# A four-layer hybrid network on one core: the head of the Mamba layer is shortened, and layer 1's contexts and queries of the first batch are computed beside the Mamba layer's scans of the second

## The chip, the core and the metric

The kernel runs on one core of a Trainium2 chip, in fp32 but for a few index matrices. The metric is the device time of one execution in microseconds (us), as the median of several runs. A profile of one further execution says where that time goes: TensorE is PE (its weight loads PEld), VectorE is DVE, ScalarE is ACT, GpSimd is POOL, and SP is the queue that starts most of the DMAs.

## What is computed

The input is x with 2 batches of 256 channels and 48 by 48 pixels, so each batch is a sequence of 2304 tokens. Four layers follow one another. Only the first two bear on this change:

```
layer 0:  h = layernorm(x) + pos;  xi, z = split(h @ in_proj)          # 512 channels each
          for each direction (forward, backward over the tokens):
            xs = silu(conv4(xi));  dt, B, C = xs @ xproj;  dt = softplus(dt @ dtproj + b)
            h_t = exp(dt_t * A) * h_(t-1) + dt_t * xs_t * B_t          # 16 states a channel
            y_t = <h_t, C_t> + D * xs_t
          x = x + ((y_f + y_b) * silu(z)) @ out_proj
layer 1:  t = groupnorm(x)                                            # over a whole batch
          q, k, v = t @ Wqkv + bqkv;  q = relu(q) / sqrt(32);  k = relu(k)
          ctx = k^T v  per head of 32 channels, over all tokens of the batch
          img = q @ ctx;  t = bn(t + proj(depthwise_conv3x3(img)))
          x = x + bn(t + mlp(t))                                      # 256 -> 2048 -> 256
```

Layer 2 is an attention and a graph-gated mixture of experts, and layer 3 is an attention and a routed mixture of experts. Neither is touched.

## The kernel before, in words

Everything lies channels by tokens: 128 partitions, two or four blocks of channels, and tokens in chunks of W = 384, six chunks to a batch. The residual `xres` stays in SBUF for the whole kernel.

**Layer 0** (`layer0`, L165 to L520) is a list `order` of 24 steps: batch 0 forward chunks 0 to 5, batch 0 backward 5 to 0, then the same for batch 1. I call them scans 0 to 23 after the function `scan` (L409) that does one. A scan goes over 4 blocks of channels and 16 states, 64 pairs in all. For each pair ACT makes exp(dt * A) in PSUM (L454), DVE runs the recurrence (L460 forward, L463 backward), DVE or POOL multiplies by C (L468), and PE adds the product into `yp` by a matmul with the identity (L422). POOL makes dt * xs * B for four states at once (L437), from `bb` and `cc`, which are broadcast from DRAM (L432, L434). The last value of each recurrence is copied into `state` (L470).

Before a chunk can be scanned, two things must have been done:

- `project_in(b, c)` (L204): layernorm of the chunk, position added, eight output blocks projected. Four go to `xi_d` in DRAM (L245), four to `z_d` (L247). It is a generator with 12 yields.
- `prepare(b, s, c, got)` (L288): loads the chunk with its neighbours from `xi_d` (L293, tile `xw`), does the short convolution as 16 matmuls with diagonal taps (L302), silu (L312), the projection to dt, B and C (L318), softplus as Abs and Relu, Exp, Ln and three additions on DVE (L335 to L348), and dt * xs on POOL (L350). It has 15 yields and hands its tiles over in `got`.

After a backward chunk, `project_out` (L354) multiplies by `w_out` and adds to `xres`. All of this is given to `scan` as `beside`, a list of (generator, steps, end): after every second pair, which is a slot (32 slots a scan), the generator is advanced so that `steps` of its yields are done by slot `end`. What the program writes is not yet the order of the queues: the builder puts each engine's instructions in an order of its own before the run, by the place in the program as a priority, and lets later work go ahead where earlier work isn't ready by its reckoning. The trace shows it: the statistics of batch 1 (L137), which stand in the program behind layer 1's fourth chunk, ran at 2441.7 us, at layer 1's start.

Beside scan i run `prepare` for scan i+1 (15 steps by slot 25), and in scans 0 to 9 also `project_in` of the chunks (0,2) to (1,5). In scans 10 to 21 there are instead three steps each of `head_products` (L367), products of layer 2's weights that only need PE and a little DVE; its 36 steps load weights (L377), multiply (L383, L397) and evacuate (L388, L390, L403 to L406). In scan 13 `group_stats` (L128) computes batch 0's groupnorm statistics. While scans run, all these helpers take their PSUM from `hold` (L199), which is one single buffer, tag "mm".

Before the first scan there is a head: `project_in` of chunks (0,0) and (0,1) in full, then `prepare` of the first chunk in full (L494 to L499). All twelve chunks of x are loaded at the start.

**Layer 1** (`layer1`, L544) does batch 0 and then batch 1. For each batch: `group_norm` (L592), the contexts over 18 token blocks (L608 to L621: K and V by PE, bias by DVE, relu by ACT, product into `cx`), then `image(c)` (L627: queries, and queries times context into the padded image `img`), `conv` (L646, nine taps on DVE), `project` (L664) and `mlp` (L683) for each chunk. `image` runs three chunks ahead. DVE fills its idle time there with `sort_list` (L895), which sorts layer 2's edges and belongs to nothing in layer 1.

Of the kernel before, what the change touches and what calls it, by code (L numbers as in the profile page):

```python
# [27 lines left out]
P = 128  # L28
# [4 lines left out]
W = 384  # L33
# [19 lines left out]
class Env:  # L53


    def __init__(self, ctx, tc, p):
        nc = self.nc = tc.nc
        self.tc, self.p, self.n_pools = tc, p, 0
        const = ctx.enter_context(tc.tile_pool(name="const", bufs=1))
        self.const = const  # L60
        self.dram = ctx.enter_context(tc.tile_pool(name="dram", bufs=1, space=DRAM))
        self.vec = const.tile([P, _NV], F32, name="vec")
        nc.sync.dma_start(self.vec, p["vecs"])
        self.ident = const.tile([P, P], F32, name="ident")
        make_identity(nc, self.ident)
        self.mean_c = const.tile([P, P], F32, name="mean_c")
        nc.vector.memset(self.mean_c, 1.0 / C)
        self.eps = {}
        for e in (1e-5, 1e-6):
            t = const.tile([P, 1], F32, name=f"eps{len(self.eps)}")  # L70
            nc.vector.memset(t, e)
            self.eps[e] = t
        self.xres = const.tile([P, 2, T], F32, name="xres")

        self.gmat = const.tile([P, P], F32, name="gmat")
        with tc.tile_pool(name="envw", bufs=1) as wp:
            same_block(self, wp, self.gmat, 3, 1.0 / 8)
        self.gn = const.tile([P, NB, 2, 2], F32, name="gn")

        self.gm_d = self.dram.tile([3, 2, P, 2 * C], F32, name="gm_d")  # L80
        self.ub = const.tile([P, 3, 2, 2], F32, name="ub")
# [45 lines left out]

def group_stats(E, wp, bank, b):  # L128

    nc = E.nc  # L130
    xb = E.xres[:, :, b * L : (b + 1) * L]
    gm, gr = E.gn[:, b, 0], E.gn[:, b, 1]
    mv = wp.tile([P, 2, 2], F32, tag="mv", name="mv")
    for k in range(2):
        st = wp.tile([P, NCH, 6], F32, tag="st", name="st")
        for c in range(NCH):
            nc.vector.bn_stats(st[:, c, :], xb[:, k, c * W : (c + 1) * W])  # L137
            yield
        nc.vector.bn_aggr(mv[:, k, :], st)
# [16 lines left out]
def load_x(E, b, c):  # L156
    xin = E.p["x"].rearrange("b (k p) n -> p b k n", p=P)
    E.nc.sync.dma_start(
        E.xres[:, :, b * L + c * W : b * L + (c + 1) * W], xin[:, b, :, c * W : (c + 1) * W]
    )  # L160
# [4 lines left out]
def layer0(ctx, E):  # L165
# [24 lines left out]
    nc.sync.dma_start(w_in, p["in_proj_wT"].rearrange("(k p) m -> p k m", p=P))  # L190
# [62 lines left out]
    for b in range(NB):  # L253
        for c in range(NCH):
            if (b, c) != (0, 0):
                load_x(E, b, c)
# [31 lines left out]
    def prepare(b, s, c, got):  # L288
# [39 lines left out]
        dt = wp.tile([P, DB, W], F32, tag="dt", name="dt")  # L328
        ex = up.tile([P, DB, W], F32, tag="ex", name="ex")
        for d in range(DB):  # L330
            pd = hold()
            nc.tensor.matmul(
                pd, lhsT=w_dt[s][:, d * P : (d + 1) * P], rhs=pr[0:16, :], start=True, stop=True
            )
            nc.scalar.activation(ex[:, d, :], pd, AF.Abs, bias=E.v(f"dt_b_{s}", d, 1))  # L335
            nc.scalar.activation(dt[:, d, :], pd, AF.Relu, bias=E.v(f"dt_b_{s}", d, 1))
            yield
        nc.scalar.activation(ex, ex, AF.Exp, scale=-1.0)
        dtu = wp.tile([P, DB, W], F32, tag="dtu", name="dtu")
        ln = up.tile([P, DB, W], F32, tag="ln", name="ln")  # L340
        nc.scalar.activation(dtu, ex, AF.Identity, bias=one[:, 0:1])
        yield
        nc.scalar.activation(ln, dtu, AF.Ln)
        nc.scalar.activation(dtu, dtu, AF.Identity, bias=one[:, 1:2])
        yield
        nc.vector.tensor_tensor(ex, ex, dtu, ALU.subtract)
        nc.vector.tensor_tensor(dt, dt, ln, ALU.add)
        nc.vector.tensor_tensor(dt, dt, ex, ALU.add)  # L348
        yield
        nc.gpsimd.tensor_tensor(dtu, dt, xs, ALU.mult)  # L350
        got.extend((b, s, c, xs, y, dt, dtu, bcd))
        yield
# [14 lines left out]
    def head_products():  # L367
# [3 lines left out]
        for h, m, z in [(h, m, z) for h in range(3) for m in range(2) for z in range(2)]:  # L371
# [35 lines left out]
            yield  # L407

# [85 lines left out]
    for steps in (first, project_in(0, 1)):  # L494
        for _ in steps:
            pass
    ready = []
    for _ in prepare(0, "f", 0, ready):
        pass  # L499
    scanning = True  # L500
    pieces = [(0, c) for c in range(2, NCH)] + [(1, c) for c in range(NCH)]
    after = None
    heads = head_products()
    for i, (b, s, step, c) in enumerate(order):
        now, ready = ready, []
        beside = [(after, 2, 5)] if after else []
        if i + 1 < len(order):
            nb, s2, _, c2 = order[i + 1]
            beside.append((prepare(nb, s2, c2, ready), 15, 25))
        if i < len(pieces):  # L510
            beside.append((project_in(*pieces[i]), 12, 32))
        elif i < len(pieces) + 12:
            beside.append((islice(heads, 3), 3, 32))
        if (b, s, step) == (1, "f", 1):

            beside.append((group_stats(E, up, lambda: hold()[:, 0:2], 0), 15, 32))
        scan(step, beside, *now)
        after = project_out(b, c, now[4]) if s == "b" else None
# [25 lines left out]
def layer1(ctx, E, edges):  # L544
# [4 lines left out]
    HD, NTB = 32, L // P  # L549
# [11 lines left out]
    wfc1 = big.tile([P, 2, 2048], F32, name="wfc1")  # L561
    nc.sync.dma_start(wfc1, p["Wfc1"].rearrange("(k p) m -> p k m", p=P))
    wfc2 = big.tile([P, 16, C], F32, name="wfc2")
    nc.sync.dma_start(wfc2, p["Wfc2"].rearrange("(k p) m -> p k m", p=P))

    hmask = big.tile([P, P], F32, name="hmask")
    same_block(E, lw, hmask, 5, HD**-0.5)

# [23 lines left out]
    def group_norm(b):  # L592
        if b:
            run(group_stats(E, wp, lambda: ps.tile([P, 2], F32, tag="mm", name="pg"), b))
        xb = E.xres[:, :, b * L : (b + 1) * L]
        for k in range(2):
            nc.vector.tensor_scalar(
                E.xn[:, k, b * L : (b + 1) * L], xb[:, k, :], E.gn[:, b, 0, k : k + 1],
# [3 lines left out]
    group_norm(0)  # L602
    for b in range(NB):
# [3 lines left out]
        cx = [psc.tile([P, P], F32, tag=f"cx{m}", name=f"cx{m}") for m in range(2)]  # L607
        for t in range(NTB):  # L608
            pk = ps.tile([P, 512], F32, tag="mm", name="pk")
            for k in range(2):  # L610
                nc.tensor.matmul(
                    pk, lhsT=xn[:, k, t * P : (t + 1) * P], rhs=wqkv[:, k, C:],
                    start=k == 0, stop=k == 1,
                )
            kv = wp.tile([P, 512], F32, tag="kv", name="kv", bufs=3)
            nc.vector.tensor_tensor(kv, pk, bkv, ALU.add)
            nc.scalar.activation(kv[:, :C], kv[:, :C], AF.Relu)
            for m in range(2):
                nc.tensor.matmul(
                    cx[m], lhsT=kv[:, m * P : (m + 1) * P], rhs=kv[:, C + m * P : C + (m + 1) * P],  # L620
                    start=t == 0, stop=t == NTB - 1,  # L621
                )
        cxm = wp.tile([P, 2, P], F32, tag="cxm", name="cxm")
        for m in range(2):
            nc.vector.tensor_tensor(cxm[:, m, :], cx[m], hmask, ALU.mult)

        def image(c):  # L627
# [97 lines left out]
        for c in range(3):  # L725
            image(c)
        t1 = project(0, conv(0))
        for c in range(NCH):
# [15 lines left out]
            if b + 1 < NB and c == NCH - 3:  # L744
                group_norm(b + 1)
# [1262 lines left out]
```

## Time and profile before

| what | us |
|---|---|
| median of the 3 runs shown (5373.67 to 5379.39) | 5376.03 |
| the profiled execution's own time | 5420.46 |
| its span, first to last instruction | 5418.6 |
| head: start to the first recurrence (L460) | 103.9 |
| scans 0 to 23: first recurrence to the last `y` (L427 starts 2426.6) | 2323 |
| layer 1: first context matmul (L611) to the last L710 | 2438.4 to 3132.1 |
| of it contexts of batch 0 and of batch 1 (L611) | 2438.4 to 2481.2, 2789.9 to 2836.0 |

In the profile's page, PE is busy for 88% of the span, DVE 65%, POOL 44%, ACT 44%. Read as one number for the whole kernel that says little: by slices, DVE and POOL are at 8 and 9 tenths during the scans (slices 1 to 17), POOL is idle in layer 1, and PE is at 9 tenths and above from there on. A matmul's end in this profile is modelled, so a busy PE isn't a PE at its peak. Weight loads overlap the matmuls.

### The profile page before, as it was taken

The page shows a single profiled execution, that of the slowest core. Times are in us where ns is not written, and L with a number is a line of the kernel's source. Part 1 is how long each engine was busy: PE and PEld are TensorE (multiplying, and loading weights), DVE is VectorE, ACT ScalarE, POOL GpSimd, SP SyncE. Part 2 cuts the span into 40 slices and gives each one's busy share as a digit, 9 for nine tenths or more (in the row PEclk, how much of TensorE's full clock was granted, in tenths as well). Part 3 has the DMA queues.
Part 4 walks back from the last instruction along what each step waited for, and adds up shares of the span by engine and source line. Part 5 has one row for each costly group of instructions (what it writes and reads, how often), then busy time and mean ns, then how long its engine had stood idle before and what let it go on. Part 6 is the DMA issues. An engine that isn't in the chain of part 4 may idle for free. (4 is left out here: it accounts for less than half of the span.)

```text
span 5418.6 us, 47326 instructions
## 1 busy us (share of the span) xinstructions
PE 4773.2 (88%) x15246; PEld 2642.9 (49%) x15246; DVE 3503.3 (65%) x5372; ACT 2370.0 (44%) x4939; POOL 2403.7 (44%) x1308
## 2 busy tenths in 40 slices
PE   7888888888787778879999989999799999999897
PEld 3444444444343344435555555556455455555675
DVE  4999888898999888899996244546534401212343
ACT  5767767666677666642223223422122222222111
POOL 2888888788888888880000000038502100000331
PEclk8999999999899899989999999999898999999899
DMA  4454454444454444431110000111121200000422
GB/s 152 166 177 173 164 178 170 159 162 151 160 174 158 173 166 158 148 137 61 33 45 6 1 16 0 40 29 30 15 72 52 61 7 9 6 9 6 83 83 94
DMA packets 185425, 499.13 MB, mean 92 GB/s; under 512 B 33382, under 2 KB 106474, under 8 KB 184906
## 3 DMA queue, kind: packets, MB, share of 16 engines
q1 hardware_dynamic: 176458, 483.23, 26.1%
q0 software_dynamic: 8704, 12.73, 1.6%
q8 instruction: 124, 2.03, 0.2%
q14 instruction: 139, 1.14, 0.1%
HBM read 422.73 MB, written 73.15 MB: 92 GB/s over the span
## 5 line engine op out<-in xcount | busy, mean ns | idle before, releaser
L422 PE MATMUL yp<-hc,ident 128*128 128x384 f32 x3072 | 1201.7, 523 | 253.2 <-DVE hc L468 210.9
L437 POOL TENSOR_TENSOR db<-dtu,bb 128x1536 f32<-128x1536 f32 x384 | 1329.1, 3462 | 64.6 <-DVE hs L463 21.0
L422 PEld LDWEIGHTS yp<-hc,ident 128*128 128x128 f32 x3072 | 576.2, 199 | 830.2 <-DVE hc L468 408.5
L468 POOL TENSOR_TENSOR hc<-ho,cc 128x384 f32<-128x384 f32 x576 | 584.9, 1023 | 189.9 <-DVE ho L460 82.6
L468 DVE TENSOR_TENSOR hc<-hs,cc 128x384 f32<-128x384 f32 x960 | 496.7, 537 | 57.9 <-PE yp L422 56.6
L454 ACT ACTIVATE hs<-dt,negab 128x384 f32<-128x384 f32 x768 | 435.9, 581 | 93.9 <-DVE hc L468 43.1
L454 ACT ACTIVATE hs<-dt,negaf 128x384 f32<-128x384 f32 x768 | 433.7, 581 | 65.0 <-DVE ho L460 28.8
L463 DVE TENSOR_TENSOR_SCAN hs<-hs,state,db 128x384 f32<-128x384 f32 x400 | 393.8, 1006 | 50.2 <-POOL db L437 23.8
L460 DVE TENSOR_TENSOR_SCAN hs<-hs,state,db 128x384 f32<-128x384 f32 x400 | 395.3, 1007 | 27.4 <-POOL db L437 19.6
L1813 POOL DMA_INDIRECT xe<-xt_d,token x48 | 47.4, 988 | 754.4 <-issue 715.3
L302 PE MATMUL mm<-xw,w_cv 128*128 128x384 f32 x768 | 292.4, 520 | 60.2 <-DVE xres L364 22.0
L1748 PE MATMUL po<-at,xtok 128*128 128x384 f32 x864 | 329.7, 506 | 8.2 <-ACT at L1746 8.1
L953 POOL PARTITION_ALL_REDUCE most<-most x1 | 0.4, 381 | 721.4 <-DVE mx L811 721.4
L1739 PE MATMUL sp<-qT,xn 128*128 128x384 f32 x864 | 317.2, 486 | 0.0
L1746 ACT ACTIVATE at<-sp 128x384 f32<-128x384 f32 x216 | 104.8, 491 | 473.1 <-PE sp L1739 473.0
L1395 PE MATMUL ph<-xn,w 128*128 128x384 f32 x768 | 287.0, 515 | 16.8 <-DMA y_d<-y 5.9
L1399 ACT ACTIVATE hid<-ph,vec 128x384 f32<-128x384 f32 x192 | 110.6, 581 | 337.2 <-PE ph L1395 244.6
L691 PE MATMUL pf<-t,wfc 128*128 128x384 f32 x768 | 255.3, 488 | 0.0
L710 PE MATMUL po<-hid,wfc 128*128 128x384 f32 x768 | 253.6, 486 | 0.0
L470 ACT COPY state<-hs 128x1 f32<-128x1 f32 x800 | 117.7, 155 | 293.6 <-DVE hc L468 291.7
L463 DVE TENSOR_TENSOR_SCAN ho<-hs,state,db 128x384 f32<-128x384 f32 x240 | 238.9, 995 | 10.3 <-ACT hs L454 10.2
L460 DVE TENSOR_TENSOR_SCAN ho<-hs,state,db 128x384 f32<-128x384 f32 x240 | 238.6, 994 | 7.0 <-ACT hs L454 6.6
(442 smaller groups left out, 7970.5 us busy)
## 6 DMA issues: line engine op xcount, KB each, us to landing
bb<-bcd SPq DMA_DIRECT2D x192, 768.0 KB
cc<-bcd SPq DMA_DIRECT2D x192, 768.0 KB
xw<-xi_d SPq DMA_DIRECT2D x24, 774.0 KB
w<-in_m_w SPq DMA_DIRECT2D x16, 1024.0 KB
y_d<-y SPq DMA_DIRECT2D x32, 384.0 KB
ye<-y_d SPq DMA_DIRECT2D x32, 384.0 KB
xi_d<-xz SPq DMA_DIRECT2D x48, 192.0 KB
z_d<-xz SPq DMA_DIRECT2D x48, 192.0 KB
```

The costliest lines, as they stand in the source:

```text
L302: nc.tensor.matmul(px, lhsT=w_cv[b, s][:, d * 4 + k, :], rhs=xw[:, d, o : o + W], start=k == 0, stop=k == 3,)
L422: nc.tensor.matmul(yp[d], lhsT=E.ident, rhs=hc, start=False, stop=summed[d] == NS)
L437: nc.gpsimd.tensor_tensor(db, bc(dtu[:, d, :], [P, GN, W], 1), bb, ALU.mult)
L454: nc.scalar.activation(hs, dt[:, d, :], AF.Exp, scale=nega[s][:, d * NS + n : d * NS + n + 1])
L460: nc.vector.tensor_tensor_scan(to, hs, db[:, j], init, ALU.mult, ALU.add)
L463: nc.vector.tensor_tensor_scan(to[:, ::-1], hs[:, ::-1], db[:, j, ::-1], init, ALU.mult, ALU.add)
L468: (nc.gpsimd if on_pool else nc.vector).tensor_tensor(hc, to, cc[:, j, :], ALU.mult)
L691: nc.tensor.matmul(pf, lhsT=wfc1[:, k, f * P : (f + 1) * P], rhs=t1[:, k, :], start=k == 0, stop=k == 1,)
L710: nc.tensor.matmul(po[m], lhsT=wfc2[:, f, m * P : (m + 1) * P], rhs=hid[:, i, :], start=f == 0, stop=f == 15,)
L1395: nc.tensor.matmul(ph, lhsT=w1[:, e, k, f * P : (f + 1) * P], rhs=xn[:, k, c * W : (c + 1) * W], start=k == 0, stop=k == 1,)
L1739: nc.tensor.matmul(sp, lhsT=xn[:, k, t0 + i * P : t0 + (i + 1) * P], rhs=qT[:, k, c * W : (c + 1) * W], start=k == 0, stop=k == 1,)
L1748: nc.tensor.matmul(po[m], lhsT=xtok[:, i, m * P : (m + 1) * P], rhs=at, start=i == 0, stop=i == MT - 1,)
```

## The change

In layer 0's head, only the xi half of `project_in(0, 0)` is run, then `prepare` of the first chunk up to the point at which two of the four channel blocks are ready. `prepare` gets a parameter `parts`, by which its softplus end is done in halves. The rest of the first `prepare` runs beside scan 0 (6 steps by slot 6). The z half of chunk (0,0), `project_in(0, 1)` and the following ones run beside the scans: in scans 0 to 4 chained in front of the `prepare` that needs them (31 or 27 steps by slot 29), in scans 5 to 10 on their own as before. The second half of `w_in` and x's other chunks are loaded later, each x chunk behind a one-column copy that depends on the current scan's dt.

The groupnorm statistics are taken piece by piece behind `project_out` (`piece_stats`), and `group_stats` only combines them. `head_products` is followed by the new generator `contexts`, both at nine steps a scan from scan 11 on. `contexts` computes layer 1's contexts of batch 0, and then its queries times context, which it writes to DRAM (`qc_d`). In layer 1 the contexts of batch 1 come first; batch 0's image is filled from `qc_d` by POOL copies (`fetch`), and batch 1's by the old code (`second`).

```
+def piece_stats(E, b, c):
+    for k in range(2):
+        at = b * L + c * W
+        E.nc.vector.bn_stats(E.st[:, b, k, c, :], E.xres[:, k, at : at + W])
+        yield
...
-def load_x(E, b, c):
+def load_x(E, b, c, after=None):
...
+    if after is not None:
+        E.nc.vector.tensor_copy(dst[:, :, 0:1], after[:, 0:2, 0:1])
+    E.nc.sync.dma_start(dst, xin[:, b, :, c * W : (c + 1) * W])
...
-    def prepare(b, s, c, got):
+    def prepare(b, s, c, got, parts=1):
...
+        n = DB // parts
+        for d0 in range(0, DB, n):
+            ds = slice(d0, d0 + n)
+            for d in range(d0, d0 + n):
...
+            nc.gpsimd.tensor_tensor(dtu[:, ds], dt[:, ds], xs[:, ds], ALU.mult)
+            if d0 == 0:
+                got.extend((b, s, c, xs, y, dt, dtu, bcd))
+            yield
...
+    def contexts():
+        flat = w_in.rearrange("p k m -> p (k m)")
+        wqkv = flat[:, : 6 * C].rearrange("p (k m) -> p k m", k=2)
...
+        def normed(c):
+            xn = up.tile([P, 2, W], F32, tag="pos", name="xn0")
+            for k in range(2):
+                nc.scalar.activation(
+                    xn[:, k, :], E.xres[:, k, c * W : (c + 1) * W], AF.Identity,
+                    bias=off[:, k : k + 1], scale=E.gn[:, 0, 1, k : k + 1],
+                )
+            return xn
+        for c in range(NCH):
+            xn = normed(c)
+            yield
...
+            for t in range(3):
+                pk = ps.tile([P, 2 * C], F32, tag="mm", name="pk")
+                for k in range(2):
+                    nc.tensor.matmul(
+                        pk, lhsT=xn[:, k, t * P : (t + 1) * P], rhs=wqkv[:, k, C:],
+                        start=k == 0, stop=False,
+                    )
+                nc.tensor.matmul(pk, lhsT=E.mean_c[0:1, :], rhs=bkv, start=False, stop=True)
+                nc.scalar.activation(kv[t][0], pk[:, :C], AF.Relu)
+                nc.scalar.copy(kv[t][1], pk[:, C:])
+                yield
+            pc = ps.tile([P, C], F32, tag="mm", name="pc")
...
+            if c == 0:
+                nc.scalar.copy(cx, pc)
+            else:
+                nc.vector.tensor_tensor(cx, cx, pc, ALU.add)
+            yield
...
+        for c in range(NCH):
+            xn = normed(c)
+            yield
+            q = up.tile([P, 2, W], F32, tag="h", name="q")
+            for m in range(2):
+                pq = hold()
...
+                nc.scalar.activation(q[:, m, :], pq, AF.Relu, bias=E.v("bq", m, 1))
+                yield
+            qc = up.tile([P, 2, W], F32, tag="sq", name="qc")
+            for m in range(2):
+                pi = hold()
+                nc.tensor.matmul(pi, lhsT=cx[:, m, :], rhs=q[:, m, :], start=True, stop=True)
+                nc.scalar.copy(qc[:, m, :], pi)
+                if m:
+                    nc.sync.dma_start(E.qc_d[:, c], qc)
+                yield
...
-    for steps in (first, project_in(0, 1)):
-        for _ in steps:
-            pass
+    for _ in islice(first, 7):
+        pass
     ready = []
-    for _ in prepare(0, "f", 0, ready):
-        pass
+    head = prepare(0, "f", 0, ready, 2)
+    while not ready:
+        next(head)
+    nc.sync.dma_start(w_in[:, :, 512:], in_wT[:, :, 512:])
+    load_x(E, 0, 1)
     scanning = True
-    pieces = [(0, c) for c in range(2, NCH)] + [(1, c) for c in range(NCH)]
+    pieces = [(b, c) for b in range(NB) for c in range(NCH)][1:]
     after = None
-    heads = head_products()
+    heads = chain(head_products(), contexts())
+    n_late = -(-(36 + 1 + 2 * 5 * NCH) // (len(order) - 1 - len(pieces)))
     for i, (b, s, step, c) in enumerate(order):
...
+        if i == 0:
+            beside.append((head, 6, 6))
+        if i + 1 < len(pieces):
+            load_x(E, *pieces[i + 1], after=now[5])
         if i + 1 < len(order):
             nb, s2, _, c2 = order[i + 1]
-            beside.append((prepare(nb, s2, c2, ready), 15, 25))
-        if i < len(pieces):
+            follow = prepare(nb, s2, c2, ready)
+            if i < NCH - 1:
+                follow = chain(first, project_in(*pieces[i]), follow)
+                beside.append((follow, 31 if i == 0 else 27, 29))
+            else:
+                beside.append((follow, 15, 25))
+        if NCH - 1 <= i < len(pieces):
             beside.append((project_in(*pieces[i]), 12, 32))
-        elif i < len(pieces) + 12:
-            beside.append((islice(heads, 3), 3, 32))
+        elif len(pieces) <= i < len(order) - 1:
+            beside.append((islice(heads, n_late), n_late, 32))
...
-        after = project_out(b, c, now[4]) if s == "b" else None
+        after = chain(project_out(b, c, now[4]), piece_stats(E, b, c)) if s == "b" else None
...
+    def fetch(c):
+        q = wp.tile([P, 2, W], F32, tag="q", name="q")
+        nc.sync.dma_start(q, E.qc_d[:, c])
+        for m in range(2):
+            nc.gpsimd.tensor_copy(
+                img[:, m, 1 + c * RW : 1 + (c + 1) * RW, 1 : WW + 1],
+                q[:, m].rearrange("p (r w) -> p r w", w=WW),
+            )
+    run(group_stats(E, wp, lambda: ps.tile([P, 2], F32, tag="mm", name="pg"), 1))
+    group_norm(1, 0, 1)
+    for c in range(3):
+        fetch(c)
...
+        if t % 3 == 0:
+            if t // 3 + 1 < NCH:
+                group_norm(1, t // 3 + 1, 1)
+            if t >= 6:
+                group_norm(0, t // 3 - 2, 1)
...
-        for c in range(3):
+        image = second if b else fetch
+        for c in range(3 if b else 0):
             image(c)
```

## The prediction

> **What bounds the kernel now.** I read the page first, then the timeline of the head, then one row of busy times for each of the 24 scans (a scan is 64 recurrences, so its start is that of every 64th), then the waits of DVE in some scans, then the timeline of layer 1.
>
> Timeline of the head:
>
> ```profile
> 32.30 0.59 SPq L293 DMA_DIRECT2D xw<-xi_d  x1
> 42.15 13.55 PE L238 MATMUL mm<-h,w_in 128*128 128x384 f32 x32 [4.91 <-DVE h L231]
> 55.54 10.49 PE L302 MATMUL mm<-xw,w_cv 128*128 128x384 f32 x32
> 69.50 5.35 PE L318 MATMUL mm<-xs,w_xf 128*48 128x384 f32 x8 [3.47 <-ACT xs L312]
> 96.66 3.66 POOL L350 TENSOR_TENSOR dtu<-dt,xs 128x1536 f32<-128x1536 f32 x1 [94.73 <-DVE dt L348]
> 103.85 0.96 DVE L460 TENSOR_TENSOR_SCAN hs<-hs,db 128x384 f32<-128x384 f32 x1 [6.82 <-POOL db L437]
> ```
>
> It is a chain on one chunk. The convolution's input is asked for at 32.30, and PE then does chunk (0,1) until 55.5. DVE's recurrences, the stuff of this layer, begin at 103.85.
>
> Rows of single scans (PE, PEld, DVE, ACT, POOL busy): scan 1 (forward), 14 (forward), 7 (backward with `project_in`), 21 and 22 (backward, with and without three steps of head products), and a stretch of layer 1's MLP:
>
> ```profile
> 193.10:289.60 96.50, 79.57 (x224) 39.48 (x224) 89.50 (x114) 69.46 (x169) 83.38 (x43) 1.00 0.48 168
> 1477.20:1568.40 91.20, 75.40 (x222) 38.08 (x220) 82.65 (x109) 64.12 (x160) 81.00 (x42) 1.00 0.49 165
> 778.10:881.10 103.00, 89.08 (x253) 46.24 (x254) 93.64 (x121) 73.27 (x169) 84.10 (x43) 0.98 0.47 167
> 2144.90:2247.40 102.50, 86.17 (x227) 43.64 (x226) 86.91 (x117) 65.15 (x154) 81.37 (x42) 0.90 0.42 149
> 2247.40:2343.70 96.30, 78.36 (x208) 39.82 (x207) 85.41 (x114) 64.26 (x153) 81.00 (x41) 0.91 0.41 148
> 2525.00:2600.00 75.00, 74.95 (x232) 43.69 (x231) 72.42 (x147) 18.18 (x31) 0.00 (x0) 1.00 0.10 32
> ```
>
> Forward scans are DVE's (89.5 of 96.5). Backward ones are not: scan 21 has less DVE work and is 6 us longer. The waits of DVE in scan 20, its twin (102.4 long), say why:
>
> ```profile
> DVE hc L468 <- PE yp L422: 5.6, 6, 1.4
> DVE hs L463 <- ACT hs L454: 2.6, 2, 2.3
> ```
>
> Three more steps on PE (86.2 for 78.4) made the scan 6.2 longer: 0.8 us a us of PE. PE never gets above 86.5% in any scan (scan 7). In layer 1 it is simply full, so work taken from PE there is worth its whole time.
>
> **Head.** The new head leaves out chunk (0,1), the z half and half the softplus. By the trace's packets, `xw` is in at 37.3, so the convolution starts there, not at 55.5. Its 10.5 us become some 12, as PE has idled (the 32 matmuls of L238 took 12.87 after an idle start). Then 0.6 bias, 1.28 table load, 1.48 silu: 53. Before, silu ended at 69.4 and the first scan came 34.4 later. From that go 3.2 (a Sqrt with its two table loads for another chunk sat in the middle), and half of Abs/Relu (2.0), of Exp, Identity, Ln, Identity (2.6 of 6.1, some of it overlapped), of DVE's three sums (2.6) and of dtu (1.8), so 22.2 stay. First scan at 76; with about 1 for later work that is let ahead, 77. Gain **27** (20 if a Sqrt comes in between again and more goes ahead, 30 if nothing does).
>
> What leaves the head is owed to the scans. Scan 0 gets the second half of the softplus: three sums of half width, 2.9 us of DVE: **+3**. A rule speaks against this half: the Trainium skill (ScalarE: Activation LUTs, What ACT_TABLE_LOAD costs) counts 2.66 us for each switch of table, with a drain behind the load. Two more switches would be 5.3. Here the load is 1.28 and silu starts 0.01 behind it, so I count 2.6, and ACT idles 29.5 of scan 0's 89.2: nothing either way. The (0,1) layernorm and projection fit into the head's idle PE and DVE time, as those of (0,2) did before. The last `project_in` now falls into scan 10: **+5** (scan 9, which has one, took 104.3; scan 10 took 99.2).
>
> Scans 1 to 4 have the same work as before, but as one chain: chunk in, DRAM, convolution, softplus, dtu. Before, `prepare` had slots 1 to 24 to itself, and its dtu ran 73.3 us into scan 1 (266.4). Now 27 steps share 29 slots of 3 us: convolution from slot 15 (45 us), Exp at slot 25 (77), then the 13.8 us that Exp to dtu took beside scan 1: dtu at 91, done at 95, first db at 98, against a scan of 96.5. POOL is at 83 of 96 and can't catch up at once. Late by 2 to 5: I take 4 for each, **+16**. From below: 0, if PE's and ACT's gaps let the chain run ahead. From above: the chain from convolution to dtu took 38 us alone in the head (41.1 less 3.2), and ACT gives half of its time to the scan; 61 us from slot 15 make dtu end at 110, 15 late or more.
>
> Small edits: piece statistics cost two bn_stats of 0.54 for each chunk. Batch 0's stood in the scans already; batch 1's move in: **+4** (6 times 1.08, less what is covered). The one-column copies ahead of x loads are ten DVE instructions near 0.1; SP waits for them with bb and cc queued behind, but the current dt is there when a scan starts: 0 (0 to 5). w_in's second half: 0, SP and DMA idle there.
>
> **Contexts and queries in scans 15 to 21.** By layer 1's rows 4 passes of L611 take 1.72 us, so pk with its bias takes 2.6, the product (L619, 4 in 0.6) 1.8 a chunk, queries 3.9 (L633 8 in 2.6, L640 4 in 1.3): 6 x (7.7 + 1.8 + 3.9) = 80 us of PE, 41 of ACT (six copies or relus, four normalizing passes and so on at 0.4 to 0.6), 3 of DVE. PE gets 61 steps in seven scans, some 11.8 each; the three head-product steps that stood there (6.5 by their rows) move to scans 11 to 14, which get nine.
>
> To price this I use PE's 86.5% as what a scan can take. Scans 11 to 14 had 80.7, 80.1, 76.0, 75.4 of PE in 97.1, 94.2, 97.0, 91.2; with 13 more each, 108, 108, 103, 102: **+41**. Forward 15 to 17 stay under it (76 to 80 of 92): 0. Backward 18 to 21 go to 78, 89, 92, 92: lengths 100, 103, 106, 106, **+9**. Sum **+50**. ACT has 25 us to spare in these scans and covers its part.
>
> Here a rule would give another number. The Trainium skill (Perfetto Trace Analysis, Identifying the Most-Contended Engine) holds matmul busy time for a poor measure and wants weight-load time. By that, scans stand at 39 to 46%, layer 1's full PE at 58% (43.7 of 75): a quarter free, and 80 us in seven scans would fit, near 15. But scans 21 and 22 differ by 18 PE instructions and by 6.2 us. PE takes instructions in order, and all helpers share one PSUM buffer, so what blocks is order, not capacity. I stay with the row; the rule's value sets the low end.
>
> **Layer 1.** Away go one batch's contexts (2789.9 to 2836.0: 46), three images of batch 0 between its MLPs (3 x 4.3 = 13), three images and the wait for the first convolution at the start (2484.3 to 2502.4, now only L670: 14), and PE's wait at 2690 to 2700 for batch 1's statistics (9.8 <- DVE dv L147). Sum 83. New at the start: batch 1's statistics after the last `xres`; some ten small operations, 4 us of which are hidden since PE waits for weights until 2438.4, and DVE can stall behind POOL's 4.3 us memset of the image (two small DVE operations took 4.1 and 4.2 beside it): -3. POOL's twelve copies fill an idle POOL; near L468's 1.0 each, under the contexts: 0 (if DVE pays for each, 12). DVE is busy for 521 of the 678 us from 2432 to 3110; that fits into the 598 that stay, so PE is the bound still. **-80** (-70 to -88).
>
> **Sum**: -27 + 3 + 16 + 5 + 4 = +1 for the head; +50 - 80 = -30 for the contexts; -29 in all. The profiled execution took 5420.5 (span 5418.6 and 1.9 around it), 0.8% above the median of 5376.0; I take the difference over as it is: **5347**.
>
> **Rivals.**
> - *The scans hide it all*: PE's gaps swallow the moved work (+15 instead of +50), and chains aren't late (0 for 16). -27 + 3 + 5 + 4 + 15 - 80 = -80: **5296**. For it: weight loads at 45%, ACT waits little. Against: scan 21 against 22.
> - *Late preparation* (slower): in scans 1 to 4 the next chunk's dtu comes late by L, because convolution and softplus start only behind the in-projection's DRAM round trip. The sum without it is -45, so it is 4L - 45; at L = 20 (61 us and more from slot 15, and a burst of POOL behind) +35: **5411**. It decides from L = 14. For it: 13 slots now for what had 21. Against: Exp to dtu kept to 13.8 beside a scan.
> - *It doesn't save*: PE costs in the scans what it saves. In 20 of the 23 scans whose rows I took, length less PE's busy time is 14 to 18, as if every us of PE lengthened a scan by one. Then the moved work costs 80: +1 + 80 - 80, within noise: **5377**.
>
> **How the numbers follow.** Forecast 0.43, hidden 0.22, late 0.20, not saving 0.15. About 0.2% (11 us) is what a measurement can tell from no change. The forecast is faster by more than that in nearly all its width (5325 to 5365 by itself), so faster 0.63, same 0.15, slower 0.22. The range runs from 5290, with everything hidden, to 5412, late by 20.
>
> **What would show it.** First recurrence near 77. Scans 1 to 4 near 100, with POOL's dtu beyond 90 us into each. Scans 11 to 14 near 105 with PE at 86%; 15 to 17 unchanged; 18 to 21 near 104. First MLP matmul (L691) some 64 us behind the last scan's end, against 2502.4 - 2427 = 75 before; no gap in PE between the batches; layer 1 shorter by 80. I am wrong if scans 0 to 4 pass 110, if scans 11 to 14 don't lengthen, or if DVE, not PE, sets layer 1's pace once contexts are gone.

## The result, and the profile after

The changed kernel takes 5411.68 us (median of 4 runs, 5408.34 to 5414.84) against 5374.85 for the kernel before in the same session: ratio **1.0073 [1.0054, 1.0092]**, slower by some 37 us. The forecast was 5347, faster.

One caution on profiles. On one of the chips used, the kernel before takes 5420 and not 5375. The 44 us lie in layer 2's experts, which the change doesn't touch: from their first matmul to layer 3's attention, eight kernels took 871 to 882 us on that chip, and six others 830 to 834 on two other chips. The profile before has 871 there, the profile after 830. So I compare profiles only up to the end of layer 1, and medians only as ratios within one session. The profiled execution of the changed kernel took 5411.0, its span is 5408.8.

The head in the timeline after (start, length, engine, line, operation):

```profile
33.20 12.22 PE L313 MATMUL mm<-xw,w_cv 128*128 128x384 f32 x32 [7.61 <-DMA xw<-xi_d]
60.99 2.92 PE L251 MATMUL mm<-h,w_in 128*128 128x384 f32 x4 [3.87 <-ACT dt L352]
71.53 0.96 DVE L556 TENSOR_TENSOR_SCAN hs<-hs,db 128x384 f32<-128x384 f32 x1 [5.28 <-POOL db L533]
```

The head did become shorter, by 32.4 us (a second profile of the kernel before, of the first experiment below, has its first recurrence at 101.4; against that it is 29.9). But the z half (L251) did not use PE's idle time: it starts at 60.99, behind the softplus (L352).

Rows of scans after, in the columns of the rows before: scans 0, 1, 14, 16, 18, 21, then a stretch of layer 1's MLP.

```profile
71.50:184.00 112.50, 88.27 (x240) 44.85 (x240) 95.57 (x117) 79.94 (x180) 82.84 (x44) 0.92 0.42 151
184.00:291.50 107.50, 87.02 (x222) 42.95 (x223) 93.68 (x114) 69.44 (x167) 81.69 (x42) 0.87 0.43 146
1544.10:1640.20 96.10, 81.62 (x239) 42.87 (x238) 85.45 (x116) 64.29 (x158) 80.99 (x42) 0.93 0.50 170
1737.00:1838.00 101.00, 87.10 (x244) 42.36 (x244) 83.94 (x111) 75.72 (x189) 81.02 (x42) 0.97 0.44 149
1935.60:2046.90 111.30, 93.03 (x231) 46.03 (x232) 83.26 (x114) 70.49 (x169) 82.84 (x42) 0.86 0.45 153
2249.00:2350.10 101.10, 83.76 (x224) 42.29 (x223) 86.61 (x117) 67.00 (x160) 82.19 (x41) 0.93 0.44 157
2620.00:2695.00 75.00, 75.00 (x234) 44.26 (x233) 72.69 (x147) 20.13 (x32) 0.00 (x0) 1.00 0.12 40
```

The row before of scan 16:

```profile
1660.50:1752.50 92.00, 72.36 (x199) 34.10 (x198) 86.39 (x109) 70.30 (x175) 82.52 (x42) 0.96 0.50 172
```

Scan 1 does the same work as before (222 matmuls recorded, 224 before), and takes 107.5 where it took 96.5. The MLP's row is the old one. Layer 1's start in the timeline of PE:

```profile
2545.26 5.41 PE L728 MATMUL pk<-wqkv,xn 128*128 128x512 f32 x8 [1.53 <-DVE xn L699]
...
2589.99 10.50 PE L819 MATMUL pf<-t,wfc 128*128 128x384 f32 x31
```

The first MLP matmul comes 58.7 us behind the last `y` (2531.3), where it was 75, and the last MLP ends at 3165.4. The budget against the profile before, a minus for time saved:

| stretch | measured, us | forecast |
|---|---|---|
| head, to the first recurrence | -32 | -27 |
| scan 0 | +23 | +3 |
| scans 1 to 4 | +43 | +16 |
| scans 5 to 9 | +6 | 0 |
| scan 10 | +6 | +5 |
| scans 11 to 14 | +25 | +41 |
| scans 15 to 17 | +22 | 0 |
| scans 18 to 21 | +9 | +9 |
| layer 1 | -71 | -80 |
| scans 22 and 23 | +2 | 0 |
| piece statistics | in the scans | +4 |
| sum, to the last MLP's end | +33 | -29 |

So the gains came nearly as forecast, and the scans gave back more than both. The 6 us of scans 5 to 9 were not followed up.

### The profile page after: what moved, and what is told of

It reads as the page before. It is cut to its first block, busy times and chain, and to the rows that moved or that the text cites. A ratio compares the mean times of both kernels' runs of the same rounds, so it can differ in the third digit from the quotient of the medians.

```text
span 5408.8 us, 47494 instructions
## 1 busy us (share of the span) xinstructions
PE 4814.1 (89%) x15282; PEld 2670.3 (49%) x15282; DVE 3516.5 (65%) x5391; ACT 2398.1 (44%) x4993; POOL 2409.9 (45%) x1321
## 5 line engine op out<-in xcount | busy, mean ns | idle before, releaser
L518 PEld LDWEIGHTS yp<-hc,ident 128*128 128x128 f32 x3072 | 588.9, 201 | 762.7 <-DVE hc L564 306.8
L564 POOL TENSOR_TENSOR hc<-ho,cc 128x384 f32<-128x384 f32 x576 | 579.3, 1013 | 220.1 <-DVE ho L559 83.9
L313 PEld LDWEIGHTS mm<-xw,w_cv 128*128 128x128 f32 x768 | 149.5, 201 | 201.6 <-ACT xs L317 35.1
```

The costliest lines, as they stand in the source:

```text
L313: nc.tensor.matmul(px, lhsT=w_cv[b, s][:, d * 4 + k, :], rhs=xw[:, d, o : o + W], start=k == 0, stop=k == 3,)
L518: nc.tensor.matmul(yp[d], lhsT=E.ident, rhs=hc, start=False, stop=summed[d] == NS)
L564: (nc.gpsimd if on_pool else nc.vector).tensor_tensor(hc, to, cc[:, j, :], ALU.mult)
```

## Experiments

All ratios are to the kernel before, run beside each other.

**The kernel before again.**

> The kernel before, unchanged. Its profile of before has a span of 5418.6 while the unprofiled median is 5375; the kernel after has 5408.8 and 5412. Up to the end of layer 1 the profile after is 33 us behind, and only between the first expert matmul of layer 2 and the start of layer 3 (untouched code) does it gain 41. Theory: those 41 belong to that one execution, not to the change. Then this run has a ratio of 1.000, and a profile in which that stretch takes near 805 us, not 842. Rival: the change does shorten layer 2, by what it leaves in memory or in the queues; then the stretch takes 842 here too.

0.9997 [0.9991, 1.0004]. The stretch in layer 2 took 874 us here too, so it was no accident of one execution, as I had thought; in later runs it went with the chip, not with the kernel.

**The two halves of the change, each alone.** The first is the kernel before with the new head and its chained steps (no `contexts`, layer 1 as before); the second has the old head and in the scans from 10 on

```
...
-        elif i < len(pieces) + 12:
-            beside.append((islice(heads, 3), 3, 32))
+        elif i < len(order) - 1:
+            beside.append((islice(heads, n_late), n_late, 32))     # n_late = 8
```

with `contexts` and the new layer 1.

> The head's half of the change alone, with head products, statistics and layer 1 as before. Late preparation: the first recurrence stays near 71.5, scans 0 to 4 stay at 108 to 112 as in the full change, scan 10 lengthens by 5: -32 + 23 + 44 + 5, slower by some 35 to 45 us (ratio 1.007 to 1.008). Rival (the contexts are what costs): the head's half is a gain of 20 to 30 us and the scans 0 to 4 are long only through something the contexts brought.

> The contexts' half alone, with the old head; heads and contexts at eight steps a scan from scan 10 on. By the measured budget (layer 1 -71, scans 11 to 22 +57) this is faster by some 10 to 20 us (ratio 0.996 to 0.998). Rival (PE's work costs in the scans what it saves in layer 1): within 0.2% of before.

Head alone 1.0071 [1.0058, 1.0085], some +38 us. Contexts alone 0.9927 [0.9913, 0.994], -40 us, a larger gain than the 10 to 20 that I had expected. The head is the half that loses: -30 to -33, by the profile of before that is taken, then +23 in scan 0 and +43 in scans 1 to 4. But the halves don't add to +37: some 39 us come only with both. Scans 11 to 18 took 754.3 in the kernel before (its second profile), 786.0 with the contexts alone, 811.5 in the full change. There the chained `project_in` reaches scan 10, so the contexts start one scan later and take 9 steps a scan, not 8.

**Why are scans 1 to 4 longer? First idea: the pace.** `beside.append((follow, 31 if i == 0 else 27, 24))` in place of 29.

> The full change with one number changed: the chained steps of scans 0 to 4 are to be done by slot 24, not 29, so each step is given earlier by a sixth. Late preparation through the pace: scans 1 to 4 go from 107.5 to about 98 to 100 and the kernel gains 30 to 40 us on the full change, ending at the time of before. Rival (late preparation through the chain's own length, or simply more work): the scans stay at 105 to 108 and the kernel within 10 us of the full change.

1.0063 [1.0049, 1.0077]; scans 1 to 4 took 103.5, 107.6, 107.6 and 106.5. When the steps are issued was not what held them back. This idea fell. Its trace shows that the loss can also lie inside the scan. In scan 2, DVE in order of time:

```profile
380.15 1.02 DVE L556 TENSOR_TENSOR_SCAN hs<-hs,state,db 128x384 f32<-128x384 f32 x1
381.64 4.64 DVE L360 TENSOR_TENSOR ex<-ex,dtu 128x1536 f32<-128x1536 f32 x1 [0.47 <-ACT dtu L358]
...
388.35 1.92 DVE L556 TENSOR_TENSOR_SCAN hs<-hs,state,db 128x384 f32<-128x384 f32 x2
```

The chain's sums stand in DVE's queue between two recurrences of the running scan, which wait with them: 8.2 us from one recurrence to the next. The next scan's first db is done at 396.6, 2 us before that scan begins, so there it is not the next scan that waits.

**Second: the round trip through DRAM.** The kernel leaves one dependence out, and so computes something else with the same work: forward chunks of batch 0 convolve the window one chunk earlier, so that nothing waits for the chunk just projected.

```
+        if b == 0 and fwd and c > 0:
+            t0 -= W
```

> The full change, but the forward convolutions of batch 0's chunks 1 to 5 read the window one chunk earlier, so they don't depend on the in-projection of the same scan (part of the computation is thereby changed; all work stays). Theory data: scans 1 to 4 last 107.5 because dtu must wait for in-projection, DRAM round trip and convolution in a row. Then they fall to 96 to 99 and the kernel to about 1.000 of before. Theory bank: all helpers take their one PSUM buffer in the order of the program, so the convolution of the next chunk stands behind the eight projection blocks whether it depends on them or not. Then scans 1 to 4 stay above 104 and the ratio above 1.005. Theory load: the scans have more work; nothing changes either.

1.0057 [1.0045, 1.0069]; scans 1 to 3 took 107.5 each, to the tenth as before the edit. The window of scan 2's convolution is now loaded in the middle of scan 1, and the convolution still starts 45.4 us into scan 2 (which begins at 292.4), as in the changed kernel:

```profile
251.10 0.54 SPq L306 DMA_DIRECT2D xw<-xi_d  x1
...
337.77 2.74 PE L315 MATMUL mm<-xw,w_cv 128*128 128x384 f32 x8
```

The data isn't what the convolution waits for.

**Third: the one PSUM buffer.** In the full change and, in the next run, with the contexts alone:

```
-    psh = ctx.enter_context(tc.tile_pool(name="l0ps_h", bufs=5, space=PSUM))
-    ps = ctx.enter_context(tc.tile_pool(name="l0ps_s", bufs=1, space=PSUM))
+    psh = ctx.enter_context(tc.tile_pool(name="l0ps_h", bufs=4, space=PSUM))
+    ps = ctx.enter_context(tc.tile_pool(name="l0ps_s", bufs=2, space=PSUM))
```

> The full change with two PSUM buffers for the helpers and four instead of five for the exponentials. Theory bank: the chain of helpers runs ahead, scans 0 to 4 lose 4 to 10 us each, scans 11 to 18 lose 2 to 5 each: 40 to 80 us faster than the full change (ratio 0.993 to 1.000). Theory data or load: scans 0 to 4 keep 105 or more; with one exponential less ahead of DVE they may even grow.

> The contexts' half alone, with two PSUM buffers for the helpers and four for the exponentials. In the contexts alone, scans 11, 12 and 16 to 18 are 4 to 7 longer than before. Theory bank (PE, in order, waits until ACT has emptied the one buffer): they shrink by 3 to 6 each, and the other scans by 1 to 3: 30 to 60 faster than the contexts alone. Rival (PE's work itself): within 10 us of it, or slower, as ACT is one exponential less ahead.

0.9976 [0.9968, 0.9984] and 0.9896 [0.9881, 0.991]. That looks like the cause, until the control: the same two lines in the kernel before.

> The kernel before with one line changed: two PSUM buffers instead of one for the helper steps beside the scans, four instead of five for the state matmuls. Theory 'the single buffer slows any work beside the scans': the kernel before gains as well. Between the contexts alone with one and with two buffers the start of scan 23 moved from 2371.3 to 2349.4 us, 22 us, of which the scans before the contexts (0 to 10) gave some 14. So 10 to 20 us, ratio 0.996 to 0.998, with scans 7 to 10 near 101 where they were 103 to 104. Rival 'the single buffer only hurts what the change adds': nothing, ratio 0.999 to 1.001.

0.9953 [0.994, 0.9966]: 25 us come from the buffers without any of the change (29 by the medians). Over that, the full change loses 0.9976 / 0.9953 = 1.0023 with two buffers, where it loses 1.0073 with one. So the buffer explains some 27 us of the loss (19 by the medians), not all; scans 2 and 3 still took 102.4, where the kernel before with two buffers takes 97.8 and 98.0. And the contexts gain no more with two buffers (0.9896 / 0.9953 = 0.9943) than with one (0.9927): the second buffer gives them some 17 us, where I had expected 30 to 60.

With three buffers for the helpers and three for the state matmuls (the contexts alone):

> The contexts alone with three PSUM buffers for the helper steps and three for the state matmuls. With two and four the ratio was 0.9896. If the helpers still queue for a buffer: 0.987 to 0.989. If the state matmuls, which then have three buffers, become what waits: scans above 100 us each from the first, ratio over 0.992. Between these, nothing is told.

0.9945 [0.9932, 0.9957]: worse than two and four, but not in the way I named. Scans 1 to 3 kept to 97.5 to 97.8; scans 7 to 9 went from 101 to 105. Which wait does it wasn't found.

**Fourth: one serial chain.** Scan 0 takes the projections of chunks 1 and 2, and from then on a projection runs one chunk ahead, beside the preparation and not in front of it. (Scan 10 has no projection left, so the contexts get 8 steps from there on; the loads of x move one chunk ahead as well.)

```
...
-            if i < NCH - 1:
-                follow = chain(first, project_in(*pieces[i]), follow)
-                beside.append((follow, 31 if i == 0 else 27, 29))
+            if i == 0:
+                follow = chain(first, project_in(*pieces[0]), follow, project_in(*pieces[1]))
+                beside.append((follow, 43, 32))
...
-        if NCH - 1 <= i < len(pieces):
-            beside.append((project_in(*pieces[i]), 12, 32))
+        if 0 < i < len(pieces) - 1:
+            beside.append((project_in(*pieces[i + 1]), 12, 32))
```

> The full change, but scan 0 carries the projections of both chunk 1 and chunk 2, so that from scan 1 on a projection runs one chunk ahead of the preparation beside it, as in the kernel before, instead of in one chain with it. The number of steps in scans 1 to 4 is the same 27 in both. Theory 'the serial chain': scans 1 to 4 go back to 96 to 99 us each with dtu near 75 us into the scan; scan 0 takes what the head left out, 130 to 145 us; contexts at 8 steps a scan behave as with the contexts alone; the sum against before is head -30, scan 0 +45, scans 1 to 4 nil, scans 5 to 22 some +27, layer 1 -71: ratio 0.992 to 0.998. Rival 'the load': scans 1 to 4 stay above 104 and the ratio is 1.004 or more.

0.9957 [0.9943, 0.9971], of which some 25 us are won in scans 11 to 18 (786.9), which have the 8 steps here. Scans 2 and 3, the same 27 steps of the same work:

```profile
292.10:391.20 99.10, 81.88 (x229) 39.64 (x229) 90.97 (x115) 70.02 (x170) 83.17 (x42) 1.00 0.47 168
391.20:488.40 97.20, 79.53 (x226) 39.39 (x225) 90.19 (x115) 69.48 (x170) 83.19 (x42) 1.00 0.48 171
```

This is the cause for scans 1 to 4: neither the load, nor the data, but the program order, in which the projection stands in front of the preparation in one chain. The one buffer makes that order dearer: with two it costs 4.5 us a scan (102.4 against 97.9), not 11. POOL's waits in scan 1 of the changed kernel (us in total, times, longest; dtu is dt * xs, and db its product with B, which the recurrence needs):

```profile
POOL dtu L364 <- DVE dt L362: 11.6, 1, 11.6
```

and its timeline there:

```profile
283.69 3.42 POOL L364 TENSOR_TENSOR dtu<-dt,xs 128x1536 f32<-128x1536 f32 x1 [11.57 <-DVE dt L362]
...
288.02 6.81 POOL L533 TENSOR_TENSOR db<-dtu,bb 128x1536 f32<-128x1536 f32 x2
```

The next chunk's dt is late, POOL stands still, and the first db ends at 291.4; scan 2 starts at 291.5. Where the wait falls can differ (in the run with the steps by slot 24 it fell on the running scan), but it is this chain that is waited for. With a projection one chunk ahead the same line of POOL in scan 2 shows no wait:

```profile
367.30 3.43 POOL L364 TENSOR_TENSOR dtu<-dt,xs 128x1536 f32<-128x1536 f32 x1
```

That is 75 us into the scan; in the changed kernel it is 99.7. Scan 0, at 116.0, paid only 3.5 for the second projection, and scan 1 (104.1) the rest; I had expected 130 to 145 for scan 0.

**Scan 0.** In the next run the contexts and the old order of the scans are kept, and only the head is reordered (and the loads of x spread over the scans): the first half of the first softplus, then the z half and `project_in(0, 1)`, and the softplus's second half beside scan 0.

```
...
+    for _ in islice(first, 7):
+        pass
     ready = []
+    head = prepare(0, "f", 0, ready, 2)
+    while not ready:
+        next(head)
     for steps in (first, project_in(0, 1)):
         for _ in steps:
             pass
...
+        if i == 0:
+            beside.append((head, 6, 6))
```

> The contexts' half with another short head: xi half of chunk (0,0), half of its softplus, and only then its z half and chunk (0,1), still ahead of the scans in the program and with the head's five PSUM buffers; scans as before, one chunk ahead. All theories that put the loss into scans 0 to 4's chain (data or bank): first recurrence at 72 to 80, scan 0 at 90 to 97, scans 1 to 4 at 96.5, so 20 to 30 us faster than the contexts alone: ratio 0.987 to 0.990. Theory load: what leaves the head is owed, scan 0 to 4 lengthen by as much: ratio 0.992.

0.9925 [0.9912, 0.9938], as with the contexts alone. First recurrence 8.6 us earlier, at 92.3, scans 1 to 3 at 96.5 to 96.7 as expected, but scan 0 at 103.6 for 89.2, where I had expected 90 to 97: more than the head saves. So I took the halves away, `prepare(0, "f", 0, ready)` with no 2, in the full change.

> The full change with the first chunk's softplus done whole before the first recurrence, not in halves (one argument). Theory 'the second half inside scan 0 costs more than it saves' (with the head reordered by itself scan 0 took 103.6 against 89.2): first recurrence 8 us later, near 79.5, scan 0 back from 112.5 to about 98, so 4 to 7 us faster than the full change: ratio 1.005 to 1.0065. Rival 'the projection inside scan 0 lengthens it': scan 0 stays at 108 or more and the head's 8 us are lost, ratio 1.008 to 1.009.

1.0041 [1.0028, 1.0054]. First recurrence at 78.4, 6.9 later; scan 0:

```profile
78.40:175.30 96.90, 79.36 (x211) 39.24 (x209) 83.31 (x110) 66.80 (x162) 80.83 (x42) 0.92 0.46 162
```

15.6 shorter. The halves cost 8.7 us net. One part of that is order again. PE in the changed kernel, then with the whole softplus (L348 is the softplus's product, here the fourth of four; L251 is a block of the z half; L225 begins chunk (0,1)'s layernorm):

```profile
68.14 0.91 PE L348 MATMUL mm<-pr,w_dtf 16*128 16x384 f32 x2 [2.09 <-ACT xz L256]
...
85.21 1.56 PE L225 MATMUL mm<-xres,mean_c 128*128 128x384 f32 x4 [2.21 <-ACT state L566]
```

```profile
26.50 1.56 PE L251 MATMUL mm<-h,w_in 128*128 128x384 f32 x4 [0.73 <-ACT xz L256]
...
43.04 1.45 PE L225 MATMUL mm<-xres,mean_c 128*128 128x384 f32 x4
```

With halves, PE's order there is third product, two z blocks (60.99 and 64.49), fourth product, two z blocks, layernorm. That is the order in which the program takes the one helper buffer, and it puts two z blocks and all of chunk (0,1) into scan 0. With the whole softplus the z half and chunk (0,1)'s layernorm do run in the head's idle time, well ahead of the first recurrence at 78.4. The other part is what a half does inside the scan. The timeline of the changed kernel, ACT and then DVE:

```profile
79.13 0.60 ACT L550 ACTIVATE hs<-dt,negaf 128x384 f32<-128x384 f32 x1
...
79.83 1.28 ACT L357 ACT_TABLE_LOAD   x1
81.13 0.84 ACT L357 ACTIVATE ln<-dtu 128x768 f32<-128x768 f32 x1
...
82.06 1.28 ACT L550 ACT_TABLE_LOAD   x1
83.35 0.58 ACT L550 ACTIVATE hs<-dt,negaf 128x384 f32<-128x384 f32 x1
```

```profile
79.76 0.97 DVE L556 TENSOR_TENSOR_SCAN hs<-hs,db 128x384 f32<-128x384 f32 x1 [0.32 <-ACT hs L550]
80.83 0.56 DVE L564 TENSOR_TENSOR hc<-hs,cc 128x384 f32<-128x384 f32 x1
82.00 3.35 DVE L361 TENSOR_TENSOR dt<-dt,ln 128x768 f32<-128x768 f32 x1 [0.62 <-ACT ln L357]
85.27 0.95 DVE L556 TENSOR_TENSOR_SCAN hs<-hs,db 128x384 f32<-128x384 f32 x1
```

At the scan's start ACT is only just ahead of DVE. With two table loads around one Ln, 4.2 us pass from one exp to the next; the sum on DVE takes 3.35 where the one after it takes 0.93, and from one recurrence to the next it is 5.5 us. The exp was there at 83.9; what the recurrence waited for last was the sum. How the 15.6 divide between the two parts wasn't measured.

7.7 of scan 0's 23 us are left. The kernel before had done the convolution of chunk (0,1) in the head, ending 6.5 us before the first recurrence; the changed kernel does it in scan 0, with either softplus. Before, scan 1, with a convolution inside, is 7.3 longer than scan 0, so this may be all of it; no run separates it.

**Scans 11 to 18: the ninth step.** `n_late = 8` in the full change, and the one step left over beside scan 23.

> The full change with 8 instead of 9 helper steps in each of scans 11 to 22, the one step left over beside scan 23. With 9 steps scans 11 to 18 took 811.3 us together, with the contexts alone (8 steps, from scan 10) 785.9. Theory 'the ninth step': what a scan pays grows faster than the steps, scans 11 to 18 fall to 785 to 792 and the ratio to 1.002 to 1.0035. Rival 'the head's lateness is carried on': scans 11 to 18 stay above 803 and the ratio at 1.006 or more.

1.0004 [0.9995, 1.0013], more than I had expected. Scans 11 to 18 fall from 811.5 to 781.7, while 19 to 22, which take over seven of the steps, stay (400.5, then 401.1). So 5 steps more than before (8 for 3) cost 27 us over eight scans, the piece statistics included, and the ninth alone 30. DVE's waits in scans 12 to 15, first with nine steps, then with eight:

```profile
DVE hc L564 <- PE yp L518: 17.9, 22, 2.6
DVE hs L556 <- POOL db L533: 11.5, 12, 2.5
```

```profile
DVE hs L556 <- POOL db L533: 10.3, 11, 2.3
DVE hc L564 <- PE yp L518: 6.8, 12, 0.8
```

With nine, DVE waits 11 us longer for PE to take its products, of the 16.1 that these four scans differ by. That the ninth step is what does it is shown; why it costs so much more than the eighth is not. The rows allow a reading: over the eight scans PE is busy for 613 us of 754.3 before (81%), 668 of 781.7 with eight steps (85.5%) and 689 of 811.5 with nine (85%), and no scan of before went above 86.5%. By it the first five steps found gaps (55 us of PE for 27 us of time) and the ninth none (21 for 30); no run tests it.

**The three mends together** (whole softplus, one chunk ahead, two buffers):

> The full change with three mends at once: the first softplus whole, scan 0 carrying the projections of chunks 1 and 2 so that later scans run one chunk ahead, and two PSUM buffers for the helpers with four for the state matmuls. If the three causes are apart, their gains add: contexts with two buffers 0.9896 (56 us), and from the head first recurrence at 78, scan 0 at 98 to 101 and scan 1 some 3 longer, so scan 2 starts 5 to 10 us earlier than there: 0.988 to 0.989. If the causes overlap (the second projection in scan 0 again delays the preparation for scan 1): scan 0 over 105, 0.990 to 0.992.

5307.13 us, ratio **0.9868 [0.9853, 0.9883]**, faster than both kernels by 68 and by some 105 us. Scan 0 took 97.6 from 75.6 on, so the causes are apart there. The ratio is a little better than expected. Against the contexts with two buffers the median is 9 us lower and scan 2 starts 10 earlier, but by scan 23 the profiles differ by 0.5 only, so what the mended head is worth is not settled by these two.

## Why the prediction was wrong

- **Head, -27: nearly right**, -32.4, above my 20 to 30: the window was in at 33.2, not at 37.3.
- **"The (0,1) layernorm and projection fit into the head's idle PE and DVE time": failed**, because of the halves. They ran inside scan 0 (layernorm at 17.6 us into it), behind the second half's products in the one buffer; with the whole softplus the layernorm and a part of the projection do fit. The convolution of chunk (0,1), which also left the head, had no term at all.
- **Second half of the softplus, +3: failed**; the halves cost scan 0 15.6, what they push into it included. I added DVE's three sums and said of ACT's table loads "nothing either way", because ACT idles a third of scan 0. On average it does, but not at the scan's start, where every exp is awaited. The rule on table loads, which I set aside, warned of the right place, but its size isn't what the trace shows: each load took 1.28, no drain behind it shows, and that its 5.3 us is near the 5.5 from one recurrence to the next is chance, since a sum on DVE ended that wait.
- **Scans 1 to 4, "late by 2 to 5: I take 4": the late chain was right, its size was not.** Measured 11. The convolution started 45.4 us into scan 2, where I had it (45). The term that failed is the way from there to Exp, 32 us in the forecast (45 to 77), 40.8 in the trace (86.2); dtu followed at 99.7 for 91, and its first db, the last link, ended at the scan's end, 107.4 for 98. I let each step run at its slot, but four convolution blocks and four of softplus queue for one buffer: the convolution's last block leaves it at 67.3. With two buffers Exp comes at 80.5 and the scan takes 102.4; the rest is not divided further. My own bound from above, 61 us from slot 15 to dtu's end, was nearer: it was 57.7. The rival "Late preparation" named the late dtu, but gave the DRAM round trip as the reason, which the experiment without the dependence excludes. Its 5411 was nearly met with L = 11 instead of 20, because other terms failed too: luck. By its own sum, 4L - 45, L = 11 would have given no loss.
- **One-column copies, "0 (0 to 5)": wrong in the trace.** I counted "ten DVE instructions near 0.1"; L171 took 0.17 to 4.43, median 1.77, 17 us in all. Most of it lies in the holes at the scans' ends: with a projection one chunk ahead, which keeps the copies, scans 2 and 3 are only 2.6 and 0.7 longer than before. So it decided little.
- **Scans 11 to 14, +41, and 15 to 17, 0: the cap of 86.5% held within two points, the PE time put under it did not.** The seven scans ended at 83 to 86% of PE (the fullest scan with one buffer has 88.6, in the contexts alone, and with two 90.4, in the full change). But scans 11 to 14 got 6 to 9 us more busy PE each where I had put 13, and took +25. And I spread the 80 us of contexts evenly, 11.8 to a scan, though by my own figures a chunk's K, V and product need 9.5 and its queries 3.9, and K, V and product come first: scans 15 to 17 had 83.0, 87.1 and 81.7 us of PE, not 76 to 80, and took +22. The sum, 47 for 41, was near because the two errors have opposite signs: luck.
- **Scans 18 to 21, +9: right** in sum (+9), not in place, for the same reason: scan 18 (93.0 us of PE, not 78) alone took 11.7, and 19 to 21, which have the queries, 2.4 less than before.
- **Layer 1, -80: nearly right**, -71. Start -16.5, batch 0's MLP stretch -15.3, contexts between the batches -40.0, the rest +0.9. PE stayed its bound, with one gap of 4.3 us between the batches.
- **"What blocks is order, not capacity"** is what the runs bear out in the head and in scans 0 to 4. I wrote it to price the contexts, where PE's share went up to the cap, and did not apply it to the head, where a gap in PE's busy time is no room if what should fill it stands behind something else.

## What to carry to other kernels

A chain of steps issued beside a scan is priced by when its last member ends, in program order over each in-order engine and each shared buffer, not by its busy time: the same 27 steps cost 8 to 11 us a scan more in one chain than in two that run a chunk apart. Moving the tail of a preparation into the consumer's first microseconds can cost twice what it saves (15.6 for 6.9 here): nothing is ahead yet there, and the tail takes the shared buffer in front of what could have filled the gap. And run the mend on the old kernel as well: of the some 50 us that a second buffer gave to the change, 25 to 29 were there without it.

## What the runs showed of the hardware

The granted TensorE clock fell behind a hole. Stretches of 9 us at the end of scan 2 of the changed kernel (columns as above; the granted clock is the third from the right):

```profile
372.50:381.50 9.00, 8.59 (x26) 4.58 (x25) 7.32 (x12) 7.78 (x18) 5.78 (x4) 1.00 0.46 168
381.50:390.50 9.00, 4.96 (x13) 2.42 (x12) 6.16 (x5) 6.56 (x8) 0.00 (x0) 0.87 0.02 8
390.50:399.50 9.00, 5.75 (x9) 2.57 (x9) 5.50 (x5) 5.21 (x9) 8.34 (x4) 0.50 0.42 141
```

POOL stands still, PE runs out of work, and in the next 9 us the clock is 0.50, so that nine matmuls take 5.75 us where 26 took 8.59. Scan 1 has a mean of 0.87, and 1.00 before the change. How much of the 11 us is this after-effect wasn't separated from the wait.

A DVE operation on SBUF alone can be held up by POOL, as far as times show it: L171 copied two columns at 284.39 and ended at 287.13, with POOL's dtu, which ran from 283.69 to 287.11; the sum at 82.00 ended 0.8 us behind a POOL product that ran until 84.53; and the sum L360, 4.64 us at 381.64 in the run with the steps by slot 24, beside a product of POOL, takes 1.76 in the changed kernel's scan 2 with POOL idle. The Trainium skill (GPSIMD Engine Reference, Specifications) says that GpSimd's SBUF interfaces are shared with VectorE, with contention for instructions with two SBUF inputs or in a two-port mode; the trace agrees for the sums, which have two SBUF inputs, and whether the copy ran in such a mode no view here shows.
